# Two gates and a hold: reordering the first loads of a conditional-adapter kernel

## The chip, the cores and the metric

The kernel runs on one core of a Trainium2 chip. The metric is device time in microseconds; the runs shown below are whole executions, and one more execution was taken with the hardware profiler, from which the views come. A core has a matrix engine (PE), a vector engine (DVE), a scalar engine (ACT), GpSimd (POOL) and a queue engine that only issues transfers (SP). All transfers run on the core's 16 DMA engines. In the profile q1 is the queue of the plain loads and stores that SP issues, q0 that of the gathers (indirect DMAs) that POOL issues.

## What is computed

```python
# x: (64, 64, 1024) fp32; two residual layers
x = x + einsum('bnr,bor->bno', einsum('bni,bri->bnr', x, B0[ids0]), A0[ids0])   # adapter chosen per sequence
base = einsum('btd,od->bto', x, W)                                            # 1024 x 1024
logits = einsum('btd,ed->bte', x, Wr) + 5 * one_hot(ids1)                      # 8 experts
gates  = softmax over the top 2 of logits, 0 elsewhere
x = x + base + 2 * einsum('bter,bte,eor->bto', einsum('btd,erd->bter', x, A1), gates, B1)
```

## The kernel before

The host lays x out transposed (features by tokens). The 4096 tokens are eight blocks of 512; block k's x is two tiles of 1 MB, x(k,0) and x(k,1), each of four chunks of 128 features, in tiles of the tag "q". For block 0 the word quarter below means two such chunks, 512 KB.

For each block:

- two gathers on POOL fetch the adapters' rows, gb (from B0) and ga (from A0), 512 KB each;
- `turn` transposes gb on PE (tile pt) and ACT copies it to bt;
- `project` multiplies bt with x (tile pb, 64 matmuls, half of them on x(k,0) and half on x(k,1)); DVE masks the result into bx;
- `adapt` multiplies ga and bx (tile px), and DVE adds it to x in eight steps;
- `rows` multiplies x with the experts' A1 and the router's Wr, side by side in a1_sb (tile ph); `gates` is a chain of small DVE operations; `weigh` transposes the gated rows (tile pg).

The large product with W + I is a fast (Strassen-like) scheme over pairs of blocks: seven outer products named by numbers, in ORDER (1, 2, 6, 7, 5, 3, 4), most of them split again into seven inner ones (tiles pa and pb, and pf for a third level). The first outer product of the first pair is done whole (tile pw): four groups of eight matmuls. W is loaded as 16 blocks of 256 KB, w(i,j). `add_identity` adds I to the diagonal blocks w(i,i) on DVE; sums of blocks are made on DVE and kept in HBM (s_kept) for the later pairs.

The order of all this isn't written by hand. Each step is given to a `Plan` with the engines that may do it, what it reads and writes, a priority `at` and the tiles it takes. `Plan.order` then runs a list schedule against its own model of time: a step starts when its inputs are ready, and of those that could start within 0.2 us of the earliest, the one with the lowest `at` goes first. In that model all transfers share one stream of 350 KB per us and land 1.8 us after their last byte. The result is one fixed program order per engine: each engine executes its instructions in that order and waits at each for what it needs. `behind=` only orders a step after the planned start of another; it makes no wait on the chip.

Waits that hold a load back are made in another way: a POOL copy of one column writes into the tile that will be loaded and reads what is to be waited for. The load, which writes the same tile, can then only be issued behind the copy. In before there are two such holds that concern us. In `load` (lines 363 to 395) the hold of x(0,1) reads the first chunk of x(0,0), which is itself loaded in two cuts:

```python
            pool.tensor_copy(made[t][:, 0, :1], made["x", 0, 0][:, 0, :1])
```

In `consts` (lines 309 to 327) the hold of a1_sb reads gb of block 0:

```python
            pool.tensor_copy(a1_sb[:, 0, :1], made["gb", 0][:, :1])
```

The loads of W (`load_w`, line 646), of x of block 1 and the gathers of block 1 are planned behind a1's start; b1 (the experts' B, 512 KB) too. So in program order SP issues: the ids, x(0,0) in two halves, Wr and the second ids, x(0,1), a1, w(0,0), w(0,1), x(1,0), x(1,1), the other 14 blocks of W, b1, and then the first stores to s_kept. POOL issues: gb of block 0, the hold of x(0,1), ga of block 0, the copy of Wr into a1_sb, the hold of a1_sb, gb of block 1, and, once px has freed its only buffer, ga of block 1.

Of the kernel before, what the change touches and what calls it, by code (L numbers as in the profile page):

```python
# [14 lines left out]
P = 128  # L15
# [159 lines left out]
def kernel(  # L175
# [52 lines left out]
    TB = 512  # L228
# [5 lines left out]
    HC = NC // 2  # L234
    QC = NC // 4
    QO = O // 4
# [17 lines left out]
    act, pool, sp = Pinned(tc, nc.scalar), Pinned(tc, nc.gpsimd), Pinned(tc, nc.sync)  # L254
# [6 lines left out]
    plan = Plan(slots, {"l"})  # L261
# [7 lines left out]
    def new(tag, shape, name):  # L269
        return pools[tag].tile(shape, F32, tag=tag, name=name)  # L270
# [16 lines left out]
    half = const.tile([P, 1], F32, name="half")  # L287
# [7 lines left out]
    a1_sb = const.tile([P, NC, P + E], F32, name="a1_sb")  # L295
# [11 lines left out]
    b1_sb = const.tile([P, O], F32, name="b1_sb")  # L307

    def consts():
        plan.add({"SP": 0.4}, lambda e: sp.dma_start(wr_c, wr), [], [("wr_c",)], -53, kb=8)  # L310
        plan.add(
            {"SP": 0.4}, lambda e: sp.dma_start(ids1_sb, ids1[0:1, :].to_broadcast([P, NB])),
            [], [("ids1",)], -53, kb=32,
        )

        def hold(e):

            pool.tensor_copy(a1_sb[:, 0, :1], made["gb", 0][:, :1])

        plan.add({"POOL": 0.2}, hold, [(("gb", 0),)], [("a1",)], -56)  # L320
        plan.add({"SP": 0.4}, lambda e: sp.dma_start(a1_sb[:, :, :P], a1), [], [("a1",)], -45, kb=512)
        plan.add({"SP": 0.4}, lambda e: sp.dma_start(b1_sb, b1), [], [("b1",)], -29, kb=512, behind=[("a1",)])

        def spread(e):
            pool.tensor_copy(a1_sb[:, :, P:], wr_c)

        plan.add({"POOL": 0.3}, spread, [("wr_c",)], [("wr",)], -45)
# [24 lines left out]
    made = {}  # L352

    def part(t, cs=range(HC), gs=range(NG)):
        return [(t, c, g) for c in cs for g in gs]
# [7 lines left out]
    def load(k, i, at):  # L363
        t = ("x", k, i)

        held = (k, i) == (0, 1)

        def hold(e):

            made[t] = new("q", [P, HC, TB], f"x_{k}_{i}")  # L370
            pool.tensor_copy(made[t][:, 0, :1], made["x", 0, 0][:, 0, :1])


        cuts = ((0, HC // 2), (HC // 2, HC)) if (k, i) == (0, 0) else ((0, HC),)

        def fn(c0, c1):
            if not held and c0 == 0:
                made[t] = new("q", [P, HC, TB], f"x_{k}_{i}")
            sp.dma_start(
                made[t][:, c0:c1],  # L380
                xT[(i * HC + c0) * P : (i * HC + c1) * P, k * TB : (k + 1) * TB].rearrange(
                    "(c p) t -> p c t", p=P
                ),
            )

        if held:
            plan.add(
                {"POOL": 0.2}, hold, part(("x", 0, 0), [0]), part(t), at, [("q", t)]
            )
        for c0, c1 in cuts:  # L390
            plan.add(
                {"SP": 0.5}, lambda e, c0=c0, c1=c1: fn(c0, c1),
                [], part(t, range(c0, c1)), at, [("q", t)] * (not held and c0 == 0),
                kb=256 * (c1 - c0), behind=[("a1",)] * (k == 1) + [(t, 0, 0)] * (c0 > 0),
            )
# [28 lines left out]
    def turn(k, g, at):  # L424

        pt, bt = ("pt", k, g), ("bt", k)

        def fn(e):
            made[pt] = new("l", [P, PER, P], f"pt_{k}_{g}")
            if g == 0:  # L430
                made[bt] = new("bt", [P, NC, P], f"bt_{k}")
            for c in range(PER):
                cc = g * PER + c
                pe.transpose(made[pt][:, c, :], made["gb", k][:, cc * P : (cc + 1) * P], ident)

        def out(e):
            act.copy(made[bt][:, g * PER : (g + 1) * PER, :], made[pt])

        plan.add(
            {"PE": 0.44}, fn, [(("gb", k),)] + [(bt, 0)] * g, [(pt,)] + [(bt, 0)] * (g == 0), at,  # L440
            [("l", pt)] + [("bt", bt)] * (g == 0),
        )
        plan.add({"ACT": 0.6}, out, [(pt,)], [(bt, g + 1)], at)
# [187 lines left out]
    def early(k, at):  # L631
        turn(k, 0, at)
        turn(k, 1, at)
        project(k, at + 2)
        adapt(k, 0, at + 3)
        adapt(k, 1, at + 4)
# [7 lines left out]
    w_name = {(i, j): ("w", i, j) for i in range(4) for j in range(4)}  # L644

    def load_w(i, j, at):
        t = w_name[i, j]

        def fn(e):
            made[t] = new("s", [P, QC, QO], f"w_{i}{j}")  # L650
            sp.dma_start(made[t], w[:, j * QC : (j + 1) * QC, i * QO : (i + 1) * QO])

        plan.add({"SP": 0.4}, fn, [], [(t,)], at, [("s", t)], kb=256, behind=[("a1",)])

    def add_identity(i, at):

# [610 lines left out]
    for q0, at in (((0, 0), -43), ((0, 2), -39), ((2, 0), -37), ((2, 2), -36)):  # L1267
        for i, j in ((0, 0), (0, 1), (1, 0), (1, 1)):

            load_w(q0[0] + i, q0[1] + j, at + 2 * i * (at == -43))  # L1270
    early(0, -40)
    biases()
    for i in range(4):
# [74 lines left out]
```

## Time and profile before

| what | value |
|---|---|
| runs | 516.07, 515.60, 515.04 us; median 515.6 |
| profiled execution | 514.86 us, of which the span from first to last instruction is 513.0 |
| PE busy | 499.8 us (97%) |
| DVE busy | 410.3 us (80%) |
| granted PE clock, mean | 0.999 |
| DMA, mean over the span | 214 GB/s; from 5 to 35 us at 348 GB/s or more |

The span begins with the first instruction and ends with the last; the profiled execution's own time has 1.86 us around it. In the page, an engine's share is its busy time over the span. In the chain of waits a line gives the start, the length and the work which held up what came after it. In the timeline a line gives the start, the length, the engine (SPq is SP's queue), the operation with out<-in, how often it follows in a row, and in brackets the idle time of the engine ahead of it with what released it. In the DMA view a queue's line gives packets, MB and the time that its packets took as a share of 16 engines' time.

### The profile page before, as it was taken

Reading aid. Unit: us, or ns where it says so; the run is one execution under the profiler, and the core shown is the slowest. Engines: PE = TensorE matmul, PEld = TensorE weight load, DVE = VectorE, ACT = ScalarE, POOL = GpSimd, SP = SyncE. Lnnn points to the kernel's source line nnn. Section 1 sums busy time; section 2 is a strip of 40 time slices with the busy share of each in tenths; the row PEclk is TensorE's granted clock in tenths of the full one; section 3 lists DMA queues with packets and bytes.
Section 4 is the critical chain, followed back from the end, with each engine's and each line's share of the span. In section 5 each row is a group of like instructions: output and inputs, shape, how many; then the busy total and the mean of one; then the engine's idle time right before and its main releaser. Section 6 shows DMA issues by size and latency. Waiting matters only on the chain.

```text
span 513.0 us, 9559 instructions
## 1 busy us (share of the span) xinstructions
PE 499.8 (97%) x3678; PEld 442.5 (86%) x3678; DVE 410.3 (80%) x822; ACT 75.8 (15%) x204; POOL 105.4 (21%) x175
## 2 busy tenths in 40 slices
PE   3999999999999999999999999999999999999997
PEld 2857888889888998889888998889989999999996
DVE  0788899989878777888989789874889988875964
ACT  1111100001000211111201221102301112112210
POOL 3002000020432433442233021201212120212100
PEclk9999999999999999999999999999999999999999
DMA  8999273964895648875567645972756665673023
GB/s 286 374 369 351 83 270 120 332 247 141 300 312 201 208 130 284 309 247 187 185 226 236 221 131 173 356 260 81 240 173 205 231 202 142 228 192 96 0 115 132
DMA packets 60172, 110.00 MB, mean 214 GB/s; under 512 B 5600, under 2 KB 11744, under 8 KB 60128
## 3 DMA queue, kind: packets, MB, share of 16 engines
q1 hardware_dynamic: 57824, 101.01, 58.7%
q0 software_dynamic: 2304, 8.39, 4.9%
q8 instruction: 29, 0.48, 0.4%
q14 instruction: 15, 0.12, 0.1%
HBM read 76.09 MB, written 33.29 MB: 213 GB/s over the span
## 4 chain that ended last, share of the span: by engine, by line
PE 94%; DMA 4%; DVE 1%; issue 0%; SPq 0%
PE pa L29 38%; PE pb L29 19%; PE pf L29 16%; PE ph L29 12%; PE px L29 3%; PE pw L29 3%; DMA x<-in_xT 3%; PE pt L29 2%; DMA gb<-in_b,idx 1%; PE pg L29 1%; DVE s L29 0%; DMA ids_sb<-in_ids 0%; DVE ti L29 0%; DVE u L29 0%; DVE x L29 0%
## 5 line engine op out<-in xcount | busy, mean ns | idle before, releaser
L29 PE MATMUL pa<-ti,s 128*128 128x256 f32 x432 | 102.1, 380 | 0.0
L29 PEld LDWEIGHTS pa<-ti,s 128*128 128x128 f32 x432 | 78.7, 190 | 9.3
L29 ACT COPY cp<-pf 128x128 f32<-128x128 f32 (+1 forms) x123 | 37.0, 302 | 214.4 <-PE pf L29 201.3
L29 PEld LDWEIGHTS ph<-a_sb,x 128*128 128x128 f32 x512 | 61.7, 190 | 1.5 <-issue 0.9
L29 PE MATMUL ph<-a_sb,x 128*128 128x136 f32 x512 | 62.5, 279 | 0.2 <-issue 0.2
L29 PE MATMUL pb<-ti,s 128*128 128x256 f32 x224 | 55.8, 380 | 0.0
L29 PE MATMUL pa<-x,s 128*128 128x256 f32 x216 | 52.7, 381 | 0.0
L29 PE MATMUL pf<-tt,sf 128*128 128x128 f32 x246 | 47.5, 277 | 0.0
L29 DVE TENSOR_TENSOR x<-px,x 128x512 f32<-128x512 f32 x64 | 39.9, 683 | 6.8 <-PE px L29 6.8
L29 PEld LDWEIGHTS pb<-ti,s 128*128 128x128 f32 x224 | 40.9, 190 | 4.8 <-issue 0.2
L29 PEld LDWEIGHTS pf<-tt,sf 128*128 128x128 f32 x246 | 41.4, 191 | 3.8 <-issue 0.4
L29 PEld LDWEIGHTS pa<-x,s 128*128 128x128 f32 x216 | 39.3, 190 | 5.0 <-issue 0.4
L29 PE MATMUL pa<-t,s 128*128 128x256 f32 x168 | 41.2, 380 | 0.0
L29 PEld LDWEIGHTS pa<-t,s 128*128 128x128 f32 x168 | 30.8, 190 | 3.9 <-issue 0.2
L29 POOL TENSOR_TENSOR tt<-ti 128x256 f32<-128x256 f32 x16 | 12.3, 771 | 93.5 <-PE pf L29 60.2
L29 DVE TENSOR_TENSOR o<-pa,u 128x512 f32<-128x512 f32 x32 | 22.0, 687 | 9.9 <-PE pa L29 9.6
L29 POOL TENSOR_TENSOR tt<-x 128x256 f32<-128x256 f32 x11 | 9.2, 833 | 93.9 <-PE pf L29 47.7
L29 DVE TENSOR_TENSOR o<-pb,o 128x512 f32<-128x512 f32 x35 | 23.1, 687 | 2.7 <-PE pb L29 1.9
L29 DVE TENSOR_TENSOR ti<-t 128x512 f32<-128x512 f32 x24 | 16.7, 696 | 8.4 <-PE pb L29 6.4
L29 DVE TENSOR_TENSOR ti<-x,ti 128x512 f32<-128x512 f32 x30 | 21.7, 724 | 1.2 <-PE pb L29 0.6
L29 DVE TENSOR_TENSOR o<-o,cp 128x256 f32<-128x256 f32 x46 | 19.6, 425 | 2.5
L29 POOL TENSOR_TENSOR sf<-s 128x128 f32<-128x128 f32 x27 | 14.0, 518 | 35.8 <-DMA s<-s_kept 14.5
(154 smaller groups left out, 807.6 us busy)
## 6 DMA issues: line engine op xcount, KB each, us to landing
s<-s_kept SPq DMA_DIRECT2D x147, 256.0 KB
x<-in_xT SPq DMA_DIRECT2D x15, 1024.0 KB
out_T<-o SPq DMA_DIRECT2D x30, 512.0 KB
s_kept<-s SPq DMA_DIRECT2D x28, 256.0 KB
sf<-f_kept SPq DMA_DIRECT2D x27, 256.0 KB
s_kept<-w SPq DMA_DIRECT2D x18, 256.0 KB
w<-in_w SPq DMA_DIRECT2D x16, 256.0 KB
f_kept<-sf SPq DMA_DIRECT2D x14, 256.0 KB
```

The source lines that it names most:

```text
L29: return self._tc.keep_in_program_order(f(*args, **kwargs))
```

## The change

Three things are changed in what is issued during the first 30 us.

1. The hold of x(0,1) reads the third chunk of x(0,0), that is the second half of that tile's load, where it read the first half. x(0,1) is loaded by two DMAs of 512 KB in place of one of 1 MB.
2. The hold of a1_sb reads the first chunk of x(0,1), where it read gb of block 0. All that is planned behind a1 (gb of block 1, W, x of block 1) is planned from there.
3. w(1,0), the third block of W in the order of loading, gets a hold of its own that reads x(1,0). The 13 blocks of W that come after it, and b1, are planned behind w(1,0).

```diff
         def hold(e):
 
-            pool.tensor_copy(a1_sb[:, 0, :1], made["gb", 0][:, :1])
-
-        plan.add({"POOL": 0.2}, hold, [(("gb", 0),)], [("a1",)], -56)
+            pool.tensor_copy(a1_sb[:, 0, :1], made["x", 0, 1][:, 0, :1])
+
+        plan.add({"POOL": 0.2}, hold, part(("x", 0, 1), [0]), [("a1",)], -56)
         plan.add({"SP": 0.4}, lambda e: sp.dma_start(a1_sb[:, :, :P], a1), [], [("a1",)], -45, kb=512)
-        plan.add({"SP": 0.4}, lambda e: sp.dma_start(b1_sb, b1), [], [("b1",)], -29, kb=512, behind=[("a1",)])
...
         held = (k, i) == (0, 1)
-
-        def hold(e):
-
-            made[t] = new("q", [P, HC, TB], f"x_{k}_{i}")
-            pool.tensor_copy(made[t][:, 0, :1], made["x", 0, 0][:, 0, :1])
-
-
-        cuts = ((0, HC // 2), (HC // 2, HC)) if (k, i) == (0, 0) else ((0, HC),)
+        half = HC // 2
+
+        def hold(c0, by):
+
+            def fn(e):
+                if c0 == 0:
+                    made[t] = new("q", [P, HC, TB], f"x_{k}_{i}")
+                pool.tensor_copy(made[t][:, c0, :1], made["x", 0, 0][:, by, :1])
+
+            return fn
+
+
+        cuts = ((0, half), (half, HC)) if k == 0 else ((0, HC),)
...
         if held:
             plan.add(
-                {"POOL": 0.2}, hold, part(("x", 0, 0), [0]), part(t), at, [("q", t)]
+                {"POOL": 0.2}, hold(0, half), part(("x", 0, 0), [half]), part(t), at, [("q", t)]
             )
...
     def load_w(i, j, at):
         t = w_name[i, j]
+        held = (i, j) == (1, 0)
+
+        def hold(e):
+
+            made[t] = new("s", [P, QC, QO], f"w_{i}{j}")
+            pool.tensor_copy(made[t][:, 0, :1], made["x", 1, 0][:, 0, :1])
+
+        if held:
+            plan.add({"POOL": 0.2}, hold, part(("x", 1, 0), [0]), [(t,)], at, [("s", t)])
 
         def fn(e):
-            made[t] = new("s", [P, QC, QO], f"w_{i}{j}")
+            if not held:
+                made[t] = new("s", [P, QC, QO], f"w_{i}{j}")
             sp.dma_start(made[t], w[:, j * QC : (j + 1) * QC, i * QO : (i + 1) * QO])
 
-        plan.add({"SP": 0.4}, fn, [], [(t,)], at, [("s", t)], kb=256, behind=[("a1",)])
+        plan.add(
+            {"SP": 0.4}, fn, [], [(t,)], at, [("s", t)] * (not held), kb=256,
+            behind=[("a1",)] + [(w_name[1, 0],)] * ((i, j) not in ((0, 0), (0, 1), (1, 0))),
+        )
...
             load_w(q0[0] + i, q0[1] + j, at + 2 * i * (at == -43))
+    plan.add(
+        {"SP": 0.4}, lambda e: sp.dma_start(b1_sb, b1), [], [("b1",)], -29, kb=512, behind=[(w_name[1, 0],)]
+    )
```

## The prediction

> **What bounds the kernel now.** I read the page first, then the chain of waits in order of time for the first 60 us (the diff touches only what is issued there), then the timeline of the issuing queues, then the DMA view in short windows.
>
> ```profile
> span 513.0 us, 9559 instructions
> PE 499.8 (97%) x3678; PEld 442.5 (86%) x3678; DVE 410.3 (80%) x822; ACT 75.8 (15%) x204; POOL 105.4 (21%) x175
> ```
>
> PE is busy for 499.8 of 513.0 us. Of the 13.2 us left, the waits of PE show 8.8 as one wait for the first gather at the very start, and 0.9 in three others. So a gain can only come from the opening: either PE starts earlier, or it stops less before its work runs gapless. The chain there (start, us, what):
>
> ```profile
> 3.08 5.59 DMA gb<-in_b,idx
> 8.80 1.94 PE pt L29 x8
> 10.74 3.39 PE pb L29 x64
> 14.15 0.30 DVE bx L29
> 14.50 2.07 PE px L29 x64
> 16.56 1.18 PE pt L29 x8
> 17.93 7.65 PE ph L29 x64
> 25.59 1.89 PE pb L29 x64
> ```
>
> Each later link of PE has a load that must have landed: the second half of pb (32 of 64 matmuls, from 12.38) needs all of x(0,1); px needs ga of block 0; the pt at 16.49 needs gb of block 1; ph needs a1; pb at 25.59 needs x of block 1. PE lost 0.42 us to bx and 0.19 us ahead of ph, and waited for no load after 8.8. The margins are what the change spends. The queues (start, us, what, idle and its releaser):
>
> ```profile
> 5.06 0.18 POOL L29 COPY x<-x 128x1 f32<-128x1 f32 x1 [0.87 <-DMA x<-in_xT]
> 5.27 0.38 SPq L29 DMA_DIRECT2D x<-in_xT  x1
> 5.40 0.97 POOL L29 DMA_INDIRECT ga<-in_a,idx  x1 [0.16 <-issue]
> 8.71 0.18 POOL L29 COPY a_sb<-gb 128x1 f32<-128x1 f32 x1 [1.88 <-DMA gb<-in_b,idx]
> 8.93 0.66 SPq L29 DMA_DIRECT2D a_sb<-in_a  x1
> 9.04 0.97 POOL L29 DMA_INDIRECT gb<-in_b,idx  x1
> ```
>
> Two POOL copies are gates: x(0,1) is issued 0.2 us behind the first quarter's landing, a1 and the second gather 0.2 to 0.3 us behind the first gather's. And the DMA view of 5.2 to 7.1 us, then of 7.1 to 8.4 us (packets, MB, share):
>
> ```profile
> q0 software_dynamic: 100, 0.41, 61.9%
> q1 hardware_dynamic: 326, 0.13, 24.9%
> ...
> q1 hardware_dynamic: 181, 0.37, 78.8%
> q0 software_dynamic: 44, 0.12, 22.8%
> ```
>
> q0 is the gather. By 7.1 us it had moved 0.41 of its 0.52 MB. In the same window q1 moved 0.13 MB, mostly small packets of wr_c and the ids, so x(0,1), issued at 5.27, had hardly begun: it moves its 1.05 MB from 7.1 to 11.0 (0.37, 0.44 and 0.24 MB in the windows ending at 8.4, 9.5 and 11).
>
> **The change part by part.**
>
> *x(0,1) behind the second quarter.* One POOL copy (0.18 us) keeps its kind and waits longer; x(0,1) becomes two SP issues of about 0.4 us, where SP has nothing else ready. The second quarter lands 512 KB behind the first: at the 356 GB/s of 3 to 5.2 us that is 1.5 us, so the copy goes from 5.06 to about 6.5 and the issue from 5.27 to 6.7. Queued behind that copy on POOL stand ga of block 0 (5.40 to about 7.1, the copy of wr_c, 0.24 us, now being planned ahead of it) and the a1 gate.
>
> What it gives the first gather is the disputed number. Upper bound: had the last 0.12 MB moved at the 377 GB/s of its window alone, it would be done 0.3 us after 7.1, and with the 0.3 us or so from last packets to landing (8.4 to 8.66) it lands at 7.7, a gain of 0.9 us. Lower bound: zero, if x(0,1) does not delay it. A slightly negative value is excluded: nothing is put ahead of it. Here the Trainium skill weighs in: "DMA: Bandwidth & Descriptors", section on queues, rings and completion order, says each DMA engine takes turns between queues by whole packets, of some 9 to 17 descriptors. A gather of 128 rows is 8 rows per engine, one such packet, so what has begun is not cut by the load. The rows of 5.2 to 8.4 us agree as far as they go: q0 did four fifths before the load moved at all. By equal shares the sum would be -0.9, by whole packets 0. I take 0.2 us earlier, near the rule's end, because only a fifth of the gather ever met the load.
>
> That gain is then capped. pb's second half starts at 12.38 and needs x(0,1). In before, its packets ended by 11.0; now it starts at about 8.0 (issue 6.7, then at most the 1.8 us of before, 5.27 to 7.1, and at least the 0.8 us of a store issued at 58.94 on an idle queue, whose bytes begin at 59.75; I take 1.3), and 1.05 MB at 398 GB/s end at 10.6, or 11.9 if ga's 0.52 MB falls inside. With the same lag of 0.4 it lands at 11.0 to 12.3: no stall at 12.38, but at most 0 to 0.6 us of room to run early. Value: 0.
>
> *Two loads of 512 KB for one of 1 MB.* The same page, section on bandwidth, advises 1 MiB or more per DMA and fits about 2.0 us fixed per DMA, which by itself would add 2 us. The trace speaks against that as a price here: the 256 KB loads of W run back to back at 353 GB/s (24 to 34 us) against 381 for 1 MB loads (15.5 to 21). Queued loads overlap their fixed part. Cost by the row: 7% of 2.6 us, 0.2 us at most, inside the margin above; I take 0.
>
> *ga of block 0.* Issued at 7.1, landing 7.3 us later as before: 14.4, against px at 14.50. By the gathers' own spread (5.6 to 7.8) 12.7 to 14.9: between no stall and 0.4. As x(0,1) is nearly through when it starts, I take the middle, 13.8: 0.
>
> *a1 behind the third quarter.* The gate goes from 8.71 to the third quarter's landing: 8.0, plus 0.52 MB at 398 GB/s (1.3), plus 0.4 to 0.9 of lag: about 10.2. a1 issues at 10.4, and behind the gate on POOL the second gb at 10.5 instead of 9.04. This is the one real cost. gb of block 1 landed 6.6 us after issue, at 15.64; pt needs it at 16.49. With the same latency it lands at 17.1 and PE stalls 0.6; with 5.6 at 16.1, no stall; with 7.8 at 18.3, 1.8. But those latencies were queueing: from 11 to 15.5 us the two queues moved 1.56 MB without a pause, ga's end, a1, this gather and the first W blocks. The bytes are the same now, so the gather should end close to where it did. I take 16.6: a stall of 0.1 to 0.2 us. a1 (last needed at 17.93) moves in front of that gather: 0.
>
> *W from its third block behind half of block 1.* Adds one POOL copy (0.2 us; POOL then waits for ga's slot and for nothing PE needs soon) and holds every SP issue behind it: 14 W blocks, b1 and the stores of W. x of block 1 moves until about 21.5, so w(1,0) is issued at 21 to 22 instead of 12.74, but it queued behind x(1,1) anyway; ga of block 1 (issued 16.94, 7.8 us to landing, 0.52 MB in 21 to 24 us) fills the gap. Price between 0 and about 1 us of DMA idling. First users: pw's third group of eight at 36.27, and on DVE the identity added to w(1,1) at 27.27, to w(2,2) at 33.43. The planner, whose model puts the third quarter and all behind it some 2.8 us later but W only 1.0 to 1.3 later, will now put these DVE additions ahead of the gates and of two px additions (0.64 us each). DVE may wait there 0.5 to 1.5 us; it has 0.51 us idle at 32.22, 0.98 at 40.83 and 1.32 at 52.3 to give it back, and px's second call on PE is at 39.71. I take 0.1 for PE; if the cover is gone, 1 us.
>
> Sum against the profiled execution (514.86 us: span 513.0 and 1.86 around it): the gather's -0.2 is lost again waiting for x(0,1), 0; +0.2 at pt; +0.1 from DVE: 515.2. The median shown is 515.6, 0.74 above the profiled one, so 515.9.
>
> **The rivals.** (A) The gather was slowed by the load: it lands at 7.7. For it: the wait of 8.8 us is the largest in the program. Against it: the two DMA windows. Its price is -0.6 to -0.9, capped by x(0,1) and gb of block 1: 514.7 to 515.0. (B) Slower: the second gb comes late. Place: pt at 16.49, in program order ahead of ph, so all of PE waits. For it: 1.5 us later issue against a margin of 0.85. Decides from a landing of 17.6 on; at 17.6 to 18.3 it costs 1.1 to 1.8: 516.7 to 517.4. Against it: the equal bytes. (C) Slower: W's stream restarts late and DVE, in its new order, stands still longer than its idle time covers, holding PSUM for pg at 35.84 or px at 39.71: +1 to +2, 516.6 to 517.6.
>
> **How the numbers follow.** A measurement of this kernel can tell about 0.2%, 1.0 us, from no change. Forecast, little net: 0.55, of which 0.05 is above that bound. A: 0.15; a good half of it (0.08) goes beyond the bound, which needs ga, px and the second gather to move up with pt. B: 0.18. C: 0.12. Faster 0.08; same 0.5 + 0.07 = 0.57; slower 0.05 + 0.18 + 0.12 = 0.35. The range leaves out half of A below and the far ends of B and C above: 514.9 to 517.4.
>
> **What would show it.** Right: PE's first pt at 8.6 to 8.8; pb's second half at about 12.4; a1's gate at about 10.2; pt of block 1 at 16.4 to 16.8; ph near 18.1; no wait of PE for w. Wrong: pt before 8.2 (A); pt of block 1 behind 17.5 with "DMA gb" as its releaser (B); PE idle at 30 to 45 us behind DVE (C).

## The result, and the profile after

| kernel | median, us | range, us | runs |
|---|---|---|---|
| before | 515.74 | 515.04 to 516.08 | 8 |
| changed | 518.75 | 516.62 to 519.87 | 8 |

The changed kernel is slower: its ratio to before is 1.0054, 95% interval 1.0041 to 1.0066, or 3.0 us. The forecast of 515.9 us with little net effect was wrong, and its range ended 1.4 us below the median. The profiled execution of the changed kernel took 517.53 us, of which 515.4 are the span. It lies 1.2 us below its median, as that of before (514.86) lies 0.9 below its own, so the two traces may be set side by side: the spans differ by 2.4 us.

The first lines of the page of the changed kernel:

```profile
span 515.4 us, 9566 instructions
...
PE 500.5 (97%) x3678; PEld 442.9 (86%) x3678; DVE 409.5 (79%) x822; ACT 75.8 (15%) x204; POOL 105.5 (20%) x176
...
PEclk9899999999999999999999999999999999999999
```

PE is busy 0.7 us longer, at the same number of instructions, and stands still 1.7 us longer. The waits of PE (work that waited, what it waited for, us in total, times, longest) say where:

```profile
PE pt L29 <- DMA gb<-in_b,idx: 8.9, 1, 8.9
PE pb L29 <- DMA x<-in_xT: 1.9, 1, 1.9
PE px L29 <- DVE bx L29: 0.4, 1, 0.4
PE ph L29 <- ACT bt L29: 0.3, 1, 0.3
```

The second line is new: pb waits for x(0,1). No line names w, so W's later stream costs PE nothing. The chain of waits in order of time, at the lines that answer to those of before:

```profile
6.19 0.19 POOL x L29
...
6.40 0.38 SPq L29
...
6.82 8.10 DMA x<-in_xT
...
14.96 0.80 PE pb L29 x16
...
15.78 0.30 DVE bx L29
...
16.13 3.29 PE px L29 x64
19.42 0.60 PE pt L29 x4
...
20.79 7.65 PE ph L29 x64
28.44 1.89 PE pb L29 x64
```

Before, the chain began with the first gather and PE held it from 8.80 us on. Now it runs through x(0,1), which needs 8.1 us from its second issue to its landing at 14.92. ph starts at 20.79 us in place of 17.93, 2.86 later. Step by step: pt starts 0.05 later (8.85 for 8.80); pb itself is 0.30 shorter (3.10 busy for 3.39); PE waits 1.92 for x(0,1); px takes 3.29 in place of 2.07, which is 1.22; the wait for bx is 0.03 shorter. The sum is 2.86. Some 0.45 come back later, 0.30 of it because the wait of before at 99.4 us for a load of x, which the prediction overlooked, is gone; 2.4 are left in the span.

The timeline of the queues (start, length, engine, operation, idle time and its releaser):

```profile
6.19 0.18 POOL L29 COPY x<-x 128x1 f32<-128x1 f32 x1 [2.19 <-DMA x<-in_xT]
6.40 0.89 SPq L29 DMA_DIRECT2D x<-in_xT  x2
...
7.12 0.96 POOL L29 DMA_INDIRECT ga<-in_a,idx  x1
...
12.39 0.18 POOL L29 COPY a_sb<-x 128x1 f32<-128x1 f32 x1 [4.31 <-DMA x<-in_xT]
12.60 0.65 SPq L29 DMA_DIRECT2D a_sb<-in_a  x1
13.07 0.97 POOL L29 DMA_INDIRECT gb<-in_b,idx  x1 [0.50 <-issue]
```

x(0,1) is issued at 6.40, as forecast (6.7). But the gate of a1, which the forecast put at 10.2, opens at 12.39, and the second gather of B0 (gb of block 1) is issued at 13.07 and not at 10.5. What the engines moved meanwhile stands in the stretches of the trace (stretch and length, busy time of PE, PEld, DVE, ACT, POOL, then granted PE clock, DMA share, GB/s), first of the changed kernel:

```profile
7.10:9.50 2.40, 0.65 (x3) 0.68 (x4) 0.00 (x0) 0.00 (x0) 0.96 (x1) 1.00 0.79 270
9.50:12.00 2.50, 2.50 (x35) 2.07 (x37) 0.00 (x0) 1.17 (x2) 0.00 (x0) 1.00 0.97 238
12.00:15.00 3.00, 1.04 (x35) 0.54 (x27) 0.00 (x0) 0.00 (x0) 1.15 (x2) 1.00 0.64 223
```

and then of before:

```profile
7.10:9.50 2.40, 0.70 (x4) 0.73 (x5) 0.00 (x0) 0.00 (x0) 0.64 (x2) 1.00 1.02 387
9.50:12.00 2.50, 2.50 (x34) 2.07 (x36) 0.00 (x0) 1.17 (x2) 0.51 (x1) 1.00 1.01 372
12.00:15.00 3.00, 2.58 (x60) 2.18 (x56) 0.29 (x1) 0.00 (x0) 0.00 (x0) 1.00 1.06 359
```

Read the last column and the one ahead of it. Rate times length gives 2.9 MB from 7.1 to 15 us before, and 1.9 MB after. A megabyte has not been moved by 15 us, at 360 GB/s some 2.8 us worth. (That ph begins about as much later is chance: 1.22 of its 2.86 us is px at a lower clock, see below.) From 7.1 to 9.5 us the engines are not full (0.79). From 9.5 to 12 they are full and yet move only 238 GB/s, because the packets take longer: by the trace's packet records 17 of ga's 128 rows took more than 0.4 us, up to 1.16, where in before none did and the mean was 0.16. From 12 to 15 us a third of their time is empty: a1's gate was shut until 12.39, and a1's first packet began at 14.05. The DMA view for the windows that the prediction showed of before, 5.2 to 7.1 and 7.1 to 8.4 us:

```profile
q0 software_dynamic: 74, 0.30, 43.4%
q1 hardware_dynamic: 329, 0.13, 24.7%
...
q0 software_dynamic: 70, 0.22, 42.0%
q1 hardware_dynamic: 67, 0.13, 36.8%
```

In the second of them q1 moved 0.13 MB where it had moved 0.37 before.

**The clock.** px is the same 64 matmuls. A finer cut of the stretches, of the changed kernel:

```profile
12.00:15.30 3.30, 1.34 (x43) 0.84 (x36) 0.00 (x0) 0.00 (x0) 1.15 (x2) 1.00 0.66 226
15.30:18.70 3.40, 3.01 (x60) 2.61 (x56) 0.70 (x2) 0.00 (x0) 0.00 (x0) 0.51 1.00 328
```

In 12 to 15.3 us PE was busy for 1.34 of 3.30 us; in the next 3.4 us the granted clock is 0.51, and px, most of which lies in it, takes 1.22 us longer. The Trainium skill ("TensorE: Matmul & The Clock Gate", Part 1 on the HAM clock gate) says that the clock halves after at least one idle window of some 3.4 us. Taken as a window without work it would leave px at 2.07, for PE was never idle that long; in this trace a window that was 40% busy was enough. The length of the slow stretch agrees.

The traces of the experiments tell more. In each of them the changes of the clock (the trace's clock records) lie whole multiples of 3.41 us apart, and the first falls anywhere from 10.46 to 21.48 us. So one can cut each trace into the clock's own windows. First two of e1, then two of e7:

```profile
15.93:19.34 3.41, 1.66 (x27) 1.28 (x22) 3.41 (x7) 0.81 (x2) 0.94 (x1) 1.00 1.04 380
19.34:22.75 3.41, 3.41 (x16) 3.41 (x17) 3.29 (x10) 0.26 (x1) 0.18 (x1) 0.50 1.05 395
...
17.90:21.31 3.41, 1.69 (x13) 1.52 (x14) 3.41 (x7) 1.07 (x2) 0.68 (x1) 1.00 1.04 377
21.31:24.72 3.41, 3.41 (x32) 3.41 (x31) 3.29 (x11) 0.06 (x1) 0.00 (x0) 1.00 1.04 396
```

The clock fell behind windows in which PE was busy for 0.22 us (e5), 1.00 (e3), 1.12 (e11), 1.46 (changed) and 1.66 (e1); it stayed behind every full-clock window of the opening with 1.69 us (e7) or more. In these 18 traces the line thus lies near half a window. (A slow window needs more to be the last: 1.93 us in e5 and 2.40 in e11 were not enough.) Where a wait falls in the windows is chance, so the same wait can cost a slow stretch in one execution and none in the next.

Two consequences for the comparison. The record begins with the first change to full clock (13.70 us in before, 11.92 in the changed kernel); ahead of it the views show 1.00, but pb's 64 matmuls took 3.39 us there and 1.89 at 25.59, so PE was slow there too. That pb is 0.30 shorter in the changed kernel is this chance. And px's 1.22 us is not all lost by the clock: the second gather, issued at 13.07, landed 6.0 us later, at 19.07. At full clock px would have ended at about 18.2 and PE would have stood until 19.1 or so; pt started at 19.35. By this estimate the slow stretch itself costs some 0.3 us here, and the late gather stands right behind it.

### The profile page after: what moved, and what is told of

It reads as the page before. It is cut to its first block, busy times and chain, and to the rows that moved or that the text cites. A ratio compares the mean times of both kernels' runs of the same rounds, so it can differ in the third digit from the quotient of the medians.

```text
span 515.4 us, 9566 instructions
## 1 busy us (share of the span) xinstructions
PE 500.5 (97%) x3678; PEld 442.9 (86%) x3678; DVE 409.5 (79%) x822; ACT 75.8 (15%) x204; POOL 105.5 (20%) x176
## 4 chain that ended last, share of the span: by engine, by line
PE 95%; DMA 4%; SPq 0%; DVE 0%; issue 0%; ACT 0%; POOL 0%; ACTq 0%
PE pa L29 39%; PE pb L29 20%; PE pf L29 16%; PE ph L29 12%; PE px L29 4%; DMA x<-in_xT 4%; PE pw L29 3%; PE pt L29 1%; PE pg L29 1%; SPq L29 0%; ACT bt L29 0%; DVE o L29 0%; DVE bx L29 0%; POOL x L29 0%; ACTq L29 0%
## 5 line engine op out<-in xcount | busy, mean ns | idle before, releaser
L29 PEld LDWEIGHTS px<-bx,ga 32*128 32x128 f32 x512 | 16.9, 199 | 6.3 <-issue 2.3
```

The source lines that it names most:

```text
L29: return self._tc.keep_in_program_order(f(*args, **kwargs))
```

## The experiments

In all of them the program order of every engine is that of the kernel that they start from, except for what is named (in e8 and e16 a few sums on DVE move a little too). Diffs are against the changed kernel where nothing else is said; `HOLD1` in a later diff stands for the first two lines of e1's and `GATE1` for those of e2's diff, `NOW` for e3's. The theory at the start was that x(0,1), held longer, lands late. Its rivals were the order of DVE, the split in two loads, the gate of a1 and the hold of W.

**e1, x(0,1) released by the first quarter again.** All else stays as changed.

```diff
-                pool.tensor_copy(made[t][:, c0, :1], made["x", 0, 0][:, by, :1])
+                pool.tensor_copy(made[t][:, c0, :1], made["x", 0, 0][:, 0, :1])
```

> The changed kernel with its program order on all engines kept, but the hold of x(0,1) reads the first quarter of block 0 again. In the changed profile x(0,1) was issued at 6.40 us, landed at 14.92, PE waited 1.9 us for it, and PE then ran px at half clock (3.29 us for 2.07). Theory 1 (the later issue of x(0,1) is the cause): issue near 5.3, x(0,1) lands by 12.5, no PE wait for it, px near 2.1 us; about 515.3 to 516.3 us, ratio to before 1.000. Theory 2 (the gate of a1 behind the third quarter lets the transfers run dry): x(0,1) still lands late or ph waits for gb of block 1; 517 to 519. Theory 3 (W's hold): 517.5 to 519.

Measured: 516.75 us, ratio 1.0023 (1.0011 to 1.0035). Its waits of PE and, from its timeline, a1's gate and the second gather:

```profile
PE pt L29 <- DMA gb<-in_b,idx: 11.0, 2, 9.6
PE pb L29 <- DMA x<-in_xT: 1.6, 3, 0.9
```

```profile
10.96 0.18 POOL L29 COPY a_sb<-x 128x1 f32<-128x1 f32 x1 [3.26 <-DMA x<-in_xT]
...
11.64 0.96 POOL L29 DMA_INDIRECT gb<-in_b,idx  x1 [0.50 <-issue]
```

The wait for gb is now in two places, 9.6 for the first gather and 1.4 for the second: this is rival B of the prediction. (The waits for x in the second line fall at 218 us and later; none is for x(0,1).) px starts at 14.32 as in before (14.50), so x(0,1) does no harm here; a1's gate alone makes the second gather late. This profiled execution (519.19) lies 2.4 us above the median: besides the wait, it has the slow stretch of 19.34 to 22.75, in which ph takes 9.32 us in place of 7.65.

**e2, a1 gated by the first gather again.** All else stays as changed.

```diff
-            pool.tensor_copy(a1_sb[:, 0, :1], made["x", 0, 1][:, 0, :1])
+            pool.tensor_copy(a1_sb[:, 0, :1], made["gb", 0][:, :1])
```

> The changed kernel in its program order, but the hold of a1 reads the first gather again, so a1, the second gather and all behind them are issued from 8.9 us on instead of 12.4. Theory 1: x(0,1) is ahead of a1 in its queue, so it lands as late as in the changed kernel or a little later, PE waits about 1.5 to 2.5 us for it: 517.5 to 519. Theory 2: the transfers no longer run dry, and the time returns to 515.5 to 516.5. Theory 3: 517.5 to 519.

Measured: 516.85 us, 1.0023 (1.0005 to 1.0040). x(0,1) still lands late, at 14.63, PE waits 1.3 for it and px takes 3.80. That is what px takes in e11 in a stretch of recorded half clock; here the record begins only at 21.48. Its profiled execution (518.59) lies 1.7 us above its median, so this trace overstates its waits.

**e3, no hold of w(1,0).**

```diff
-            pool.tensor_copy(made[t][:, 0, :1], made["x", 1, 0][:, 0, :1])
```

> The changed kernel in its program order, without the POOL copy that holds W's third block: w(1,0) and all behind it on SP are issued as soon as SP reaches them. Theories 1 and 2: the opening up to ph is unchanged; DVE loses its waits for w (1.2 and 2.0 us in the changed profile), PE gains nothing: 517.5 to 519.5, like the changed kernel. Theory 3: 515.5 to 516.5.

Measured: 518.68 us, 1.0059 (1.0043 to 1.0075), as the changed kernel. The hold of W costs and gives nothing.

**e4, the new order alone.** Program order of the changed kernel, but both holds read what they read before, x(0,1) is one load, and W is not held.

```diff
HOLD1, GATE1, NOW, and in load's fn:
+            if t == ("x", 0, 1):
+                if c0:
+                    return
+                c1 = HC
```

> The changed kernel's program order on every engine with before's waits: x(0,1) in one load behind the first quarter, the hold of a1 on the first gather, no hold of W. What is left of the change is the order: three identity additions earlier on DVE, the copy of Wr ahead of ga on POOL, one store ahead of w(1,0) on SP. Theories 1, 2 and 3: 515.3 to 516.2, ratio within 0.1% of 1. If the order itself is the cause: 517 or more.

Measured: 515.68 us, 1.0006 (0.9995 to 1.0017). The order, with its earlier identity additions on DVE, is worth nothing.

**e5, the hold alone.** e4 with the hold of x(0,1) on the second quarter: its diff without HOLD1.

> The program order of the changed kernel, with before's waits except one: x(0,1), in one load, is held behind the second quarter. In the profile with the gate of a1 on the first gather, the same hold and x(0,1) in two loads, x(0,1) was issued at 6.7 and landed at 14.6. Theory 1 (the later issue by itself): x(0,1) lands at 13.5 to 15, PE waits 1 to 2.5 us for it; 516.5 to 518. Theory 1b (the two loads of half the size are slow, not the hold): x(0,1) lands by 12.8, PE waits under 0.5 us; 515.5 to 516.2.

Measured: 519.08 us, 1.0044 (1.0024 to 1.0063), runs from 515.01 to 521.54. The profiled one is the slowest of them:

```profile
PE pb L29 <- DMA x<-in_xT: 5.2, 2, 4.7
```

4.7 of the 5.2 us are for x(0,1); the rest falls in a later block. One load or two, the hold makes x(0,1) late.

**e6, the split alone.** e4 with x(0,1) in two loads: HOLD1, GATE1 and NOW alone.

> The program order of the changed kernel, with before's waits, but x(0,1) in two loads of 512 KB. Theory 1: like before, 515.3 to 516.2. Theory 1b: x(0,1) lands a us or more later than in the same order with one load, 516.3 to 517.5.

Measured: 515.32 us, 0.9992 (0.9980 to 1.0004). Two loads of 512 KB cost nothing that can be measured. With e1 and e2 this closes a table of two by two, all with two loads:

| ratio to before | a1 gated by the first gather | a1 gated by the third quarter |
|---|---|---|
| x(0,1) behind the first quarter | 0.9992 (e6) | 1.0023 (e1) |
| x(0,1) behind the second quarter | 1.0023 (e2) | 1.0054 (changed) |

Each gate adds 0.0031 in either row or column, 1.6 us of 515.7, and the differences' intervals (from those of the single ratios, some 0.002 to either side) leave out zero. (e6 has no hold of W, which by e3 doesn't matter.) So half of the loss is the hold of x(0,1) and half is the gate of a1.

The clock has a part in both halves. One slow window of 3.41 us lowers an execution's mean granted clock to 0.997. In e6 none of 14 executions is at or below that, and of before's 153 beside the experiments two are. In e1 it is 7 of 22, with a median of 517.6 us against 516.2 for the other 15; in e2 7 of 22, with 518.1 against 516.2; in the changed kernel 6 of 8, with 519.1 against 517.3. The executions without a recorded slow window still rank as in the table, about 0.6 us above before in e1 and e2 and 1.6 in the changed kernel (two executions). So the waits cost by themselves, and the more of them there are, the more often the clock adds to them.

**e7, ga of block 0 ahead.** The changed kernel, but ga is issued on POOL right behind the first gather, at 4.39 us in place of 7.12.

```diff
+                made["ga", 0] = new("ga", [P, D], "ga_0")
+                pool.indirect_dma_start(
+                    out=made["ga", 0], out_offset=None, in_=a0,
+                    in_offset=bass.IndirectOffsetOnAxis(ap=idx[:, 0:1], axis=0),
+                )
...
+            if (tag, k) == ("ga", 0):
+                return
```

> The changed kernel, all its waits kept, but POOL issues the gather of ga of block 0 right behind the first gather and ahead of the copy that waits for the second quarter (issue near 4.1 instead of 7.1). Theory G (on some DMA engines the rows of ga get in ahead of x(0,1), which is why it lands late): ga is through before x(0,1), which then lands near 12 to 12.8; PE waits under 0.7 us for it; 515.8 to 517. Theory R (x(0,1) is late because engines that are done have nothing queued and start it late): it still lands after 13.8; 517.5 to 519.

Measured: 518.86 us, 1.0059 (1.0037 to 1.0081).

```profile
PE pt L29 <- DMA gb<-in_b,idx: 11.4, 2, 9.4
PE px L29 <- DVE bx L29: 0.4, 1, 0.4
```

No wait for x(0,1) is left, and the time is the same: the third quarter, behind two gathers, opens a1's gate at 12.32, and PE waits 2.0 us for the second gather. One wait has taken the other's place: at full clock throughout, ph starts at 20.68, 0.1 us earlier than in the changed kernel. (The profiled execution, 517.39, lies 1.5 us below the median.)

**e8, before with the small loads moved.** Diff against before: Wr and the second ids are issued behind x(0,1).

```diff
-        plan.add({"SP": 0.4}, lambda e: sp.dma_start(wr_c, wr), [], [("wr_c",)], -53, kb=8)
+        plan.add({"SP": 0.4}, lambda e: sp.dma_start(wr_c, wr), [], [("wr_c",)], -53, kb=8, behind=[(("x", 0, 1), 0, 0)])
...
-            [], [("ids1",)], -53, kb=32,
+            [], [("ids1",)], -53, kb=32, behind=[(("x", 0, 1), 0, 0)],
```

> Before, unchanged but for one thing: the two small loads wr_c and ids1 (32 KB each, 256 packets of 256 bytes, moved at 5.2 to 7.1 us while the first gather's rows start) are issued behind x(0,1). If they hold the first gather back: it lands at 7.8 to 8.3 instead of 8.66, PE starts earlier by as much, 514.8 to 515.4. If the gather is slow by itself: 8.6 or later, 515.4 to 516.0.

Measured: 518.97 us, 1.0067 (1.0045 to 1.0088), a clear miss. The first gather came earlier, pt starts at 8.09, but x(0,1), issued at 5.32 as in before, landed at 13.31 and PE waited 1.4 us for it. The time of issue is not the whole cause. What was new is that SP's queue ran dry ahead of x(0,1): the last packet of x(0,0) began at 5.87 and its own first one at 6.83. (The profiled execution, 515.73, is the fastest of the six, 3.2 us below their median. It shows this wait, not what makes the median.)

From here on the packets themselves were read. A load of x is 512 packets of 2 KB; the table gives when x(0,1) was issued, when its first, its 256th and its last packet began, the mean duration of its first 64, when ga was issued and when its first row began (us, durations in ns, from the trace's packet records):

| kernel | issue | first | 256th | last | first 64 | ga issued | ga's first row |
|---|---|---|---|---|---|---|---|
| before | 5.27 | 7.09 | 8.79 | 11.04 | 97 | 5.40 | 9.64 |
| e4 | 5.17 | 7.05 | 8.95 | 11.05 | 98 | 6.85 | 9.63 |
| e1 | 5.07 | 7.38 | 9.25 | 11.57 | 92 | 6.74 | 10.02 |
| changed | 6.40 | 7.43 | 9.82 | 14.31 | 118 | 7.12 | 10.50 |
| e2 | 6.69 | 7.70 | 9.86 | 14.01 | 154 | 7.04 | 10.65 |
| e3 | 7.15 | 8.18 | 10.28 | 15.16 | 110 | 7.49 | 11.00 |
| e5 | 6.49 | 7.51 | 10.08 | 16.38 | 162 | 6.82 | 10.52 |
| e7 | 6.60 | 8.72 | 10.63 | 13.04 | 87 | 4.39 | 7.99 |
| e8 | 5.32 | 6.83 | 9.05 | 12.81 | 187 | 5.45 | 8.31 |

Two things stand out. In before, x(0,1) waits in the queue behind the 256 small packets of Wr and the second ids (the last of them at 7.07) and its packets then run at their usual length from the first on. Held to the second quarter it finds at most a rest of them (nine in ten are through by 6.57 in the changed kernel), its first packet comes 1.0 us after the issue in each of the four kernels, and its first packets take a tenth to two thirds longer (97 ns before, 110 to 162). And its last packets are very late, 4.2 to 6.3 us behind the 256th, where in before, e1 and e4 it is 2.1 to 2.3. The next runs ask which of the two matters.

**e9, something in the queue.** e5 with b1's 512 KB issued at 3.14 us, right behind the ids.

```diff
-            {"SP": 0.4}, lambda e: sp.dma_start(ids1_sb, ids1[0:1, :].to_broadcast([P, NB])),
+            {"SP": 0.4}, lambda e: (sp.dma_start(ids1_sb, ids1[0:1, :].to_broadcast([P, NB])), sp.dma_start(b1_sb, b1)),
...
-        {"SP": 0.4}, lambda e: sp.dma_start(b1_sb, b1), [], [("b1",)], -29, kb=512, behind=[(w_name[1, 0],)]
+        {"SP": 0.4}, lambda e: None, [], [("b1",)], -29, kb=512, behind=[(w_name[1, 0],)]
```

> The hold on the second quarter alone (one load of 1 MB, a1 gated on the first gather, no hold of W), but with b1's 512 KB issued by SP right behind the second ids, so that SP's queue still has packets when x(0,1) is issued at about 6.5 us. Theory 1 (a load that is issued onto a queue that has run empty starts late on some of the 16 DMA engines): in spite of 0.5 MB more ahead of it, the stretch from 7.1 to 9.5 us moves 350 GB/s or more (211 with the hold alone), x(0,1) lands within 13 us instead of at 17, PE waits at most 1.5 us for it in place of 5.2, and the time falls from 519.1 to 516 to 517.5. Theory 2 (the later issue as such is what costs): b1 is 0.5 MB more in front, x(0,1) lands no earlier than with the hold alone, and the time is 519 or more.

Measured: 518.29 us, 1.0043 (1.0027 to 1.0059). 353 GB/s from 7.1 to 9.5 us and 99 ns for the first 64 packets, as the first theory said; but the 512 KB also went ahead of the first gather, pt started at 11.66 in place of 8.8, and x(0,1) landed late for its place behind them. The time that it gave, 516 to 517.5, was missed.

**e10, no hold at all.** Before, without the POOL copy: x(0,1) is issued at 3.15 us. Diff against before:

```diff
-            pool.tensor_copy(made[t][:, 0, :1], made["x", 0, 0][:, 0, :1])
```

> The kernel before without any hold on x(0,1): SP issues it at about 3.1 us, right behind the ids, so its queue never runs empty. Theory 1: x(0,1) lands near 10 us on all engines, PE never waits for it, and nothing is erratic; the price is the first gather, whose 0.52 MB now share the engines with 1.05 MB. If rows of gathers are cut in by whole packets, pt starts at 8.8 to 9.5 and the time is 515.5 to 516.5; by equal shares pt starts at 9.5 to 10.5 and the time is 516.5 to 517.5. Theory 2 (the earlier the issue the better) gives 515 to 515.7.

Measured: 518.20 us, 1.0041 (1.0025 to 1.0057). From its timeline:

```profile
13.11 1.94 PE L29 MATMUL pt<-ident,gb 128*128 128x128 f32 x8 [13.11 <-DMA gb<-in_b,idx]
```

The first gather lands 4.3 us later, more than the 2.7 us that 1.05 MB take at 387 GB/s, and more than either count of the expectation allowed. Sharing the engines does not explain it, for they had room. The stretch from 5.5 to 8.5 us, first of e10, then of before:

```profile
5.50:8.50 3.00, 0.00 (x0) 0.00 (x0) 0.00 (x0) 0.00 (x0) 0.24 (x1) 1.00 0.51 146
...
5.50:8.50 3.00, 0.00 (x0) 0.00 (x0) 0.00 (x0) 0.00 (x0) 1.11 (x2) 1.00 0.93 326
```

The gather's first row began at 6.62 in place of 5.44, and half of the engines' time was empty. Why is open; ga too was issued earlier here, at 4.30. Before's hold, on the first quarter, is worth 2 us.

**e11, ga out of the way.** e5, but ga is issued behind a1's gate, at 8.93 us in place of 6.82. On top of e5:

```diff
             pool.tensor_copy(a1_sb[:, 0, :1], made["gb", 0][:, :1])
+            made["ga", 0] = new("ga", [P, D], "ga_0")
+            pool.indirect_dma_start(
+                out=made["ga", 0], out_offset=None, in_=a0,
+                in_offset=bass.IndirectOffsetOnAxis(ap=idx[:, 0:1], axis=0),
+            )
...
+            if (tag, k) == ("ga", 0):
+                return
```

> The hold on the second quarter alone, as before with one load, a1 gated on the first gather and no hold of W, but ga of block 0 is issued only behind the gate of a1, at about 9 us instead of 6.8, so that from 6.5 to 9 us only x(0,1) and the end of the first gather are under way. Theory 1 (empty queue): the stretch from 7.1 to 9.5 us still moves under 290 GB/s and x(0,1) still lands behind 14 us on some engines. Theory 3 (the second gather's rows cut in ahead of x(0,1), which would start promptly without them): 350 GB/s or more from 7.1 to 9.5 us, x(0,1) lands by 11.5 us, and PE does not wait for it. In both, px waits for ga, which lands at about 14.5 to 16, and the second gather of B0 comes a microsecond later: the time is 517 to 520 and tells little.

Measured: 519.04 us, 1.0053 (1.0036 to 1.0071).

```profile
PE px L29 <- DMA ga<-in_a,idx: 2.9, 1, 2.9
PE pb L29 <- DMA x<-in_xT: 0.4, 1, 0.4
```

```profile
7.10:9.50 2.40, 0.82 (x4) 0.85 (x5) 0.00 (x0) 0.00 (x0) 0.93 (x3) 1.00 0.74 164
```

Each theory was half right. The start is slow without a gather beside it: 164 GB/s, first packet 1.0 us after the issue at 7.08, and the first 64, which begin from 8.09 on, behind the first gather's last row (8.06), at 237 ns. But the late end is gone: the last packet begins at 12.28 (14.01 to 16.38 in changed, e2, e3 and e5), and PE's wait for x(0,1) falls from 4.7 to 0.4 us. PE then waits 2.9 for ga instead.

**e12, small loads as cover.** Before, with Wr and the second ids issued at 4.91 and 5.30 us, behind the first quarter's landing and right ahead of x(0,1) (5.78). Diff against before, in the hold of x(0,1); the steps of the two loads issue nothing:

```diff
+            pool.tensor_copy(wr_c[:, 0, :1], made["x", 0, 0][:, 0, :1])
+            sp.dma_start(wr_c, wr)
+            sp.dma_start(ids1_sb, ids1[0:1, :].to_broadcast([P, NB]))
             pool.tensor_copy(made[t][:, 0, :1], made["x", 0, 0][:, 0, :1])
```

> The kernel before, with the small loads (Wr and the second ids) issued by SP behind the first quarter's landing, right ahead of x(0,1), which is so issued at about 6.1 us instead of 5.3. Their some 290 small packets lie in the queue when x(0,1) is issued. Theory 1 (what is still queued at the issue hides the slow start of a load): x(0,1)'s first 64 packets take about 100 ns each, 7.1 to 9.5 us moves 340 GB/s or more, the load is complete by 12.5 us and PE waits under 0.4 us for it, though it is issued 0.8 us later than before; the gather, with fewer packets in its way, lands near 8.0, and the time is 515 to 516.5. Theory 2 (time of issue): 7.1 to 9.5 us moves under 300 GB/s, PE waits 1 us or more for x(0,1), and the time is 517.5 to 519.

Measured: 518.77 us, 1.0060 (1.0039 to 1.0080), the first theory's time missed. The first gather was early (pt at 7.43), and the first 64 packets of x(0,1) took 97 ns. But ga's rows began at 6.99 and went ahead of most of x(0,1), whose last packet began at 14.34; PE waited 3.8 us for it. Small packets that are themselves just issued did not help.

**e13, the same in the changed kernel.** The same three lines in the changed kernel's hold. The copy into wr_c reads the first quarter, not the second as the expectation has it, so the small loads were issued at 5.17 and x(0,1) at 6.52.

> The changed kernel with all its waits, but the small loads issued right ahead of x(0,1), behind the second quarter's landing: about 6.4 us for the first of them, 7.3 us for x(0,1). Theory 1: the first small packets now bear the slow start and x(0,1) has its normal packets of about 100 ns and no engine is late by more than a microsecond, but it starts about 8.5 and lands at 13 to 13.5; PE waits 1 us or less for it (1.9 in the changed kernel), the gate of a1 opens at about 12, and the second gather is late as before: 517.5 to 518.5. Theory 2: the issue is 0.9 us later still, PE waits 2.5 us or more, 519.5 to 520.5.

Measured: 517.35 us, 1.0027 (1.0014 to 1.0040), faster than the changed kernel. pt starts at 7.65, ga is issued only at 8.61 (POOL stands at the copy of Wr), the last packet of x(0,1) begins at 12.27. The first 64 packets of x(0,1) took 143 ns with small packets ahead of them. PE waits in small pieces: 1.1 for x(0,1), 0.7 for ga, 2.3 ahead of the second pt. The view puts these 2.3 down to DVE; but pt's gather, issued at 12.22 behind the gate, landed at 18.42, and pt started at 18.55. Of the 22 executions the 12 with a slow window have a median of 518.1 us, the 10 others of 516.2.

**e14, the gather first.** Before, with the second quarter also held to the first quarter's landing. Diff against before, in the hold of x(0,1); the second quarter's own step issues nothing:

```diff
+            b = made["x", 0, 0]
+            pool.tensor_copy(b[:, HC // 2, :1], b[:, 0, :1])
+            sp.dma_start(
+                b[:, HC // 2 :],
+                xT[HC // 2 * P : HC * P, :TB].rearrange("(c p) t -> p c t", p=P),
+            )
             pool.tensor_copy(made[t][:, 0, :1], made["x", 0, 0][:, 0, :1])
```

> The kernel before with the second quarter also held to the first quarter's landing, so that SP issues it at about 4.6 us and x(0,1) right behind it, and the first gather meets only small packets. If the gather's rows go behind whatever plain loads are queued (as with no hold at all), they start about 0.5 to 1 us earlier, pt starts at 7.2 to 8.0, the second quarter lands near 9 and x(0,1), issued onto a queue that is not empty, near 12: PE waits 0.3 to 1 us for it, and the time is 514.8 to 515.8, at best 0.2% faster than before. If the gather needs its 2.4 us from issue to first row anyway, pt stays at 8.3 or later, both loads are later by a microsecond, and the time is 516.5 to 518.

Measured: 520.90 us, 1.0093 (1.0070 to 1.0115), the slowest. pt did start at 7.77, but both loads came later and PE waited 3.8 us for x of block 0.

**e15, e13 with a1 gated by the first gather.** e13's diff and GATE1.

> Like e13 (the changed kernel with the small loads behind the first quarter's landing, at about 5.2 us, so that the first gather has only the end of x(0,0) beside it), but a1's gate reads the first gather again. If the gate on the third quarter is what made the second gather late in e13 (issued at 12.2, PE waited 2.3 us), it is now issued at 9 to 9.7 and PE waits under 0.5 us for it; x(0,1) lands by 13 and ga by 14; ph starts at 17.2 to 18.2 in place of 20.0 and the time is 515 to 516, level with before. If the second gather instead cuts in ahead of x(0,1) and ga, PE waits 1.5 us or more for one of them, and the time is 517 or more.

Measured: 516.66 us, 1.0013 (1.0000 to 1.0026), above the forecast of the first theory.

```profile
PE pt L29 <- DMA gb<-in_b,idx: 9.3, 2, 7.8
PE px L29 <- DMA ga<-in_a,idx: 1.0, 1, 1.0
PE pb L29 <- DMA x<-in_xT: 0.9, 2, 0.6
```

The second gather is issued at 10.03, 2.2 us earlier than in e13, but takes 7.9 us to land in place of 6.2, and PE waits 1.5 us for it, where it was 2.3. (The waits for x fall behind 60 us.) The gate costs here too, by the medians 0.7 us, though the two intervals overlap.

**e16, e8 with ga behind a1's gate.** e8's diff and the lines of e11's.

> Like e8 (the kernel before with the small loads issued behind x(0,1)), but ga of block 0 is issued behind a1's gate, at about 8.2 us in place of 5.45, and the second gather of B0 a microsecond later, at about 9.2. If ga's rows beside x(0,1) are what made a few engines late with it in e8 (the last 32 packets took 1.2 us, landing at 13.3, PE waited 1.4), x(0,1) now lands by 11.5 and PE does not wait for it; px waits 0 to 1 us for ga; the time is 515 to 516.5. If the load that is issued onto an empty queue is slow by itself, x(0,1) still lands at 12.5 or later, px and the second pt wait besides, and the time is 518 or more.

Measured: 519.33 us, 1.0071 (1.0052 to 1.0090). ga's first row began at 12.94, behind all of x(0,1), and still the last packet of it began at 12.32, only 0.5 us earlier than in e8. Here the slow start is most of it, where in e11 ga's place was.

## Why the prediction was wrong, by its own steps

*The first gather.* 0.2 us earlier was taken; pt started at 8.85, 0.05 later, and rival A (7.7) did not come. Over more traces the step looks better: with the hold on the second quarter (changed, e2, e3, e5) pt starts at 8.70 to 9.02, on the first (before, e1, e4, e6) at 8.80 to 9.58; the means differ by 0.3. The reason given, that the rows of a gather once begun are not cut by a load, is not borne out by e10: there the gather's rows ran beside x(0,1)'s packets from 6.62 us on, and it landed 4.3 us later.

*x(0,1): the first step that failed.* The prediction had it start at 8.0, move at 398 GB/s and land at 11.0 to 12.3, and booked nothing. It started earlier, at 7.43, and landed at 14.92. The 398 GB/s were the rate of a full queue. In before the load queued behind small packets and ran at its usual rate from its first packet on, and it had begun four fifths of its packets when ga's first row came (9.64); in the changed kernel the queue was nearly empty, the first packets were slow, and it was two thirds, at 10.50. (That the small packets hid the start is likely but not shown: in e13 and e15 the load had them ahead of it and was slow all the same.) From the first packet to the last it took 6.9 us, 4.0 in before. This is 1.92 us of PE's wait in the trace, and by the table of two by two 1.6 us in the medians, the clock's part included. The hold also acts through the gate, which opens at 12.39 here and at 10.96 in e1.

*Two loads.* 0 was taken, against the 2.0 us fixed per DMA of the Trainium skill; e6 (0.9992) bears that out. The skill fits this figure in the section "Anatomy of one DMA" of "DMA: Bandwidth & Descriptors", not in that on bandwidth, and for DMAs that GpSimd issues; x(0,1) is issued by SP.

*ga of block 0.* 0 was taken, and PE did not wait for it. But it is what x(0,1) met (e11): its price was paid at another wait, which the step didn't look at.

*a1's gate: the second step that failed.* It should have opened at 10.2 and cost 0.1 to 0.2 us. It opened at 12.39. The third quarter was not landed when its bytes would have been through at the mean rate: half of x(0,1)'s packets had begun by 9.82, 2.6 us before the gate opened. (That some of the 16 engines were behind the others is an inference; the packet records name no engine.) "The bytes are the same now, so the gather should end close to where it did" presumed engines that never pause; from 12 to 15 us they had 0.64 of their time filled, as a1 and the second gather were issued only behind the gate. In the changed kernel's trace the late gather (landing at 19.07) hides behind the wait for x(0,1) and the slow px, so that rival B's sign, a wait of pt for gb, is not seen in it; e1 shows it bare with 1.4 us, e7 with 2.0, and the medians give the gate 1.6 us, the clock's part included. This was rival B, with a price of 1.1 to 1.8 and a chance of 0.18.

*W and DVE.* 0.1 was taken, 0 came. DVE runs the identity additions where they were predicted to go and waits for w 1.21 us at 30.5 and 1.95 us at 38.3, the second longer than the 0.5 to 1.5 expected, but nothing on PE waits for that (e3, e4). Rival C is out.

*What was not in the sum.* The clock. The sum took a wait at its own length. In the changed kernel's trace a wait of 1.92 us brought a window under half busy, and px took 1.22 us longer; e7 waited 2.0 us and kept its clock. Whether a given execution pays is a matter of where the windows fall.

So the mechanism of the likeliest case, little net, was wrong in two terms of the sum, each put at 0 to 0.2 and each worth 1.6. What stays open: why the first packets of x(0,1) are slow, why its last packets take so long beside ga's rows (from 9.5 to 12 us full engines moved only 238 GB/s, some of ga's rows taking six to seven times their usual 0.16 us), and how the loss divides between the slow start and ga. e5 against e11 gives most of it to ga, e8 against e16 to the start; both are single traces of kernels whose runs scatter by 3 to 7 us.

No version beat before. e6 is level with it (0.9980 to 1.0004). Six kernels had the first gather 0.7 to 1.4 us earlier (e8, e12 to e16: pt at 7.43 to 8.09), and none was faster: each lost it again at x(0,1), at ga or at the second gather.

## What to carry to other kernels

A hold moves more than a start: look at what stands in the queue when the load is issued and at what is issued just behind it, for here the load onto a nearly drained queue started slowly and then shared the engines with what followed. Where several loads and gathers feed one engine in a row, ask of each gate whether the DMA engines have work up to the moment when it opens; here a gate on the last link of a chain left them a third empty for 3 us. When one wait is removed, look for the next one right behind it (e7). And if waits of PE come close together, count the clock with them: less than about half of a 3.4 us window busy brought the next one to half clock.

## What was unexpected of the hardware

- A load issued by SP onto a queue that had nearly drained began 1.0 us after the start of its issue (changed, e2, e3, e5, e11: 1.01 to 1.03; 1.5 in e8 and e16), and its first 64 packets took 110 to 237 ns, against 92 to 100 in before, e1, e4, e6, e9 and e12, where packets were queued ahead. Such packets are no sure cover: in e10, e13, e14 and e15 there were some, and the first 64 took 112 to 188 ns.
- Plain loads in the queue held back gathered rows by more than their bytes: with 1 MB more queued the first gather landed 4.3 us later (e10), with 0.5 MB 2.9 us (e9), while in e10 the engines were busy for only 0.51 of their time from 5.5 to 8.5 us.
- The 256 packets of 256 bytes of Wr and the second ids, 64 KB in all, seem to hold the first gather up: with them issued later, pt started 0.7 to 1.4 us earlier (e8, e12, e13, e15, e16), out of proportion to their bytes.
- Half clock came behind windows of 3.41 us in which PE was busy for up to 1.66 us (49%), not idle, and did not come behind full-clock windows with 1.69 us or more.
